# Cross-attention and feed-forward on one core: a new plan of the background work, products four tiles behind, a constant in the eviction of scores

## The chip, the cores and the metric

The kernel runs on one core of one Trainium2 chip. The metric is the device time of one execution in microseconds. Three runs of the kernel before took 1978.9, 1977.6 and 1969.8 us, median 1977.6. Engines are named as in the profile: PE is TensorE, PEld its weight loads, DVE VectorE, ACT ScalarE, POOL GpSimd, SP SyncE, which here only issues DMAs.

## The reference, cut to what matters

1600 query rows (16 x 100) attend to 5776 context rows (16 x 361) with 16 heads of 32. Queries and keys are quantised per row and head to 127 steps, values per column, and the softmax weights per row to 255 steps. A feed-forward part with 1408 hidden columns follows; the change does not touch it.

```python
def _fq_sym(x, axis):
    s = jnp.max(jnp.abs(x), axis=axis, keepdims=True) / 127.0
    s = jnp.maximum(s, 1e-08)
    return jnp.clip(jnp.round(x / s), -127.0, 127.0) * s      # value only
...
q, k, v = _fq_sym(q * scale, -1), _fq_sym(k, -1), _fq_sym(v, 2)  # v: over all keys
attn = softmax(einsum('bhqd,bhkd->bhqk', q, k))
attn = _fq_unsigned(attn, -1)                                  # 255 steps, s = max / 255
out = einsum('bhqk,bhkd->bhqd', attn, v)
...
x = x + xattn(layernorm(x), ctx) @ Wp + bp
x = x + ffn(x)
```

Because the largest weight of a row becomes 255, the weights in steps are exp(score - max + ln 255), rounded; the row's sum of the unrounded values is kept for the division at the end. So a row's maximum over all 5776 scores must be known before its first exponential.

## The kernel before, in words

**Stages.** A prologue (to 172.8 us) normalises and projects the queries, and projects, rounds and turns the keys and values of the first four heads. Then come 200 *tiles*, 172.8 to 1705.1 us, and then the feed-forward with the rest of the output projection, to 1972.7 us. A tile is 128 queries of one head against all keys: 12 tiles a head, and a thirteenth that holds the last 64 queries of two heads (25 tiles a pair of heads, 50 a *group* of four heads). The keys are padded to 5796 = 46 blocks (`NB`) of 126 (`KB`).

**A tile.** The loop at L1148 walks over the tiles. Each has five chunks of scores (`CHUNKS`, 1536, 1024, 1536, 1024, 656 columns in an even tile, the first four swapped in an odd one). For each chunk PE multiplies into one of two PSUM buffers `sl` (L1170), and DVE evicts it into one of two SBUF buffers `score` (L1186), multiplied by the row's negative scale `nqs`, which it reads through a pointer to a column of one element per partition, while it accumulates the minimum into `mx`. POOL makes of the five minima the bias `nb` (two instructions behind the fourth chunk, L1213 and L1214, and one behind the fifth, L1220). ACT takes the exponentials in two pieces (L1129): the first `NP` = 20 blocks go as bytes, those of two blocks packed in 16 bits, into `pairc`, at the end of the tile's own turn; the other 26 blocks as `codes` one tile later, at the place that `WINDOWS` calls "turn". SP issues the two DMA transposes (L1134 into `pk`, L1137 into `rT`) right behind each. POOL unpacks `pk` into `rU` (L1141) two tiles later. PE multiplies the transposed weights with the values (`av`, L1050, 46 blocks a tile) into `oacc`, `LAG` = 3 tiles behind; where in the tile how many blocks come stands in `WINDOWS`, whose entry per chunk is (turn, units of projection, blocks). `pk`, `rT` and `rU` have 2, 3 and 2 buffers.

**Background work.** While group g runs, the keys and values of group g+1 are made. `plan_pair` (L690) puts a pair of context blocks on tiles n and n+1: four projection matmuls a tile (`unit_pe`, L252, and L254 for the bias) into `pp`, one PSUM buffer; the loads of `cb` three blocks ahead (L217); the keys' maxima `pair_max` (L264, DVE) at the end of tile n+1; the copy of `pp` to SBUF, `pair_keep` (L275, ACT), ahead of the first exponential of tile n+1; then the scale (L281, POOL), its inverse (L287, DVE) and the rounding (L292, L298, POOL). 23 pairs take the 46 first tiles of a group. `plan_keys` puts the splitting of a head's keys into three bf16 parts (L360 to L366, POOL), their transposes (L373, PE) and the copy (L377, ACT) on the tiles that `PLAN["keys"]` lists. At the end of a group the values' maxima are taken over all keys (`values_max`, L305 and L309, DVE), turned and spread (L313 to L332), and the values divided (L337, POOL) and rounded (L340, ACT) on the tiles in `PLAN["divide"]`, some of them in the next group. `values_copy` (L392, POOL) makes a head's values f16. Finished heads are scaled into `og` (L1089) and stored (L1110, L1116). The last group has no next one to project: its tiles carry the output projection instead (`part_load` to `part_store`, L721 to L752, and the loads of the feed-forward's weights, L441).

**What sets the order.** Each engine executes in the order in which the program issues to it, and the order in the loop is written out by hand: per tile the lists "pool", "turn", "pe", "dve", "act0" and "act" hold what `put` placed there. "act0" runs ahead of the second exponential of the tile before, "act" ahead of the tile's own first exponential, "dve" behind the five evictions, "pool" ahead of everything that POOL does in the tile. The DMA queues in question are ACT's (loads of `cb`, weights, `qT`) and SP's (the transposes, `store`, the prologue's loads).

Of the kernel before, what the change touches and what calls it, by code (L numbers as in the profile page):

```python
# [22 lines left out]
P = 128  # L23
C = 512
H = 16
# [6 lines left out]
NP = 20  # L32
# [7 lines left out]
LAG = 3  # L40
# [9 lines left out]
    "keys": ((1, 3, 5, 7, 9, 11), (13, 15, 17, 19, 21, 23), (25, 27, 29, 31, 33, 35), (37, 39, 41, 43, 45, 48)),  # L50
    "query": ((0, 4, 5), (14, 14, 18), (25, 27, 29), (39, 41, 43)),
    "copy": ((4, 8), (18, 20), (29, 30), (50, 50)),
    "max": (30, 31, 33, 35, 37, 41, 40, 42, 45, 46),
    "finish": (47, 48, 49),
    "divide": (49, 52, 52, 52, 52, 52, 53, 53, 53, 54, 55, 56),
    "prefetch": (46, 47, 49, 49),
    "store": (3, 6, 9, 9),
# [4 lines left out]
    "keys": ((1, 3, 5, 7, 9, 11), (13, 15, 17, 19, 21, 23), (25, 27, 29, 31, 33, 35)),  # L62
    "query": ((0, 4, 5), (14, 14, 18), (25, 27, 29)),
    "copy": ((4, 8), (18, 20), (29, 30)),
# [17 lines left out]
    ((0, 0, 2), (1, 1, 8), (0, 1, 16), (0, 1, 8), (0, 1, 12)),  # L82
    ((0, 0, 0), (1, 0, 8), (0, 2, 8), (0, 1, 20), (0, 1, 10)),
# [4 lines left out]
    ("norm", 0), ("codes", 0), ("project", 1), ("keep", 0), ("norm", 1), ("values", 3), ("codes", 1),  # L88
# [24 lines left out]
def xattn_ffn(ctx: ExitStack, tc: tile.TileContext, xin, ctxt, wq, bq, wkv, bkv, wp, bp, w13, w2, nw, out):  # L113
# [100 lines left out]
    def load(g, t):  # L214
        if g < H // G and t < NB:
            cbs[g, t] = genp.tile([P, 4, P], F32, name=f"cb_{g}_{t}", tag="cb", bufs=3)
            nc.scalar.dma_start(cbs[g, t], ctxt[:, t])  # L217

    def prefetch(g, i):

        if i < 4:
            if i == 0:
                wts_g[g] = genp.tile([P, 4, 2 * P], F32, name=f"wkv_{g}", tag="wkv", bufs=1)
            nc.scalar.dma_start(wts_g[g][:, i, :], wkv[:, g, i, :])
        if i:
            load(g, i - 1)
# [62 lines left out]
    def keys_round(g, u):  # L289
# [8 lines left out]
        nc.gpsimd.tensor_scalar(kint[g][:, 2 * u : 2 * u + 2, :], vraw[:, k : k + 2, :], MAGIC, MAGIC, ALU.add, ALU.subtract)  # L298

    def values_max(g, t0, t1, c0=0, c1=P):  # L300

        if t0 == 0 and c0 == 0:
            fin["vm"] = genp.tile([P, P], F32, name=f"vm_{g}", tag="vm", bufs=1)
        vm = fin["vm"][:, c0:c1] if t0 == 0 else genp.tile([P, P], F32, name=f"vp_{g}_{t0}", tag="vp", bufs=1)
        nc.vector.tensor_reduce(  # L305
            vm, vraw[:, t0:t1, c0:c1].rearrange("p t c -> p c t"), AX.X, ALU.max, apply_absolute_value=True
        )
        if t0:
            nc.vector.tensor_tensor(fin["vm"], fin["vm"], vm, ALU.max)  # L309

    def values_turn(g, pool):
        fin["pt"] = pool.tile([P, P], F32, name=f"vmt_{g}", tag="tr")
        nc.tensor.transpose(fin["pt"], fin["vm"], ident_f)  # L313

    def values_scale(g):
        vmx = genp.tile([P, 1], F32, name=f"vmx_{g}", tag="vmx", bufs=1)
        nc.vector.reduce_max(vmx, fin["pt"], axis=AX.X)
# [4 lines left out]
    def values_diag(g):  # L322
        fin["diag"] = genp.tile([P, P], F32, name=f"diag_{g}", tag="vm", bufs=1)
        nc.gpsimd.tensor_scalar(fin["diag"], ident_f, fin["rsv"], None, ALU.mult)

    def values_spread(g, pool):
        fin["pb"] = pool.tile([P, P], F32, name=f"rsvb_{g}", tag="tr")
        nc.tensor.matmul(fin["pb"], ones_f, fin["diag"], start=True, stop=True)

    def values_keep(g):  # L330
        fin["rsvb"] = genp.tile([P, P], F32, name=f"rsvs_{g}", tag="vp", bufs=1)
# [49 lines left out]
    def query_load(h, c0=0, c1=NQ, copies=(0, 1, 2)):  # L381

        qT[h] = qTs[h % 2]
        for r in copies:
            nc.scalar.dma_start(qT[h][r * HD : (r + 1) * HD, c0:c1], q_dram[h * HD : (h + 1) * HD, c0:c1])
# [20 lines left out]
    def values_sum_keep(h):  # L406
# [5 lines left out]
        nc.scalar.dma_start(v16[h][0:1, NP:, :], exp_["row0", h])  # L412
# [5 lines left out]
    def values_rest_keep(h):  # L418
        nc.scalar.dma_start(v16[h][1:2, NP:, :], exp_.pop(("row1", h)))
# [40 lines left out]
    with (  # L460
# [135 lines left out]
        for t in range(NB):  # L596
# [11 lines left out]
            if t % 8 == 7 or t == NB - 1:  # L608
                c0 = t // 8 * 8
                at(t + WHEN["values"], values_max, 0, c0, t + 1)  # L610
# [24 lines left out]
        at(n, values_turn, 0, pps)  # L635
# [22 lines left out]
    for s in score:  # L658
        nc.gpsimd.memset(s[:, NK:], 1e30)
# [4 lines left out]
    with tc.manual_schedule():  # L664
# [25 lines left out]
        def plan_pair(g, u, n):  # L690
# [5 lines left out]
            put(n + 1, "act", pair_keep, g, u, first=True)  # L696
            put(n + 2, "pool", keys_scale, g, u)
            put(n + 2, "dve", keys_inverse, g, u)
            put(n + (4 if 12 < n % 50 < 35 else 3), "pool", keys_round, g, u)
# [249 lines left out]
        for g in range(H // G):  # L949
# [6 lines left out]
            if g == 0:  # L956
                put(2, "act", query_load, h, 8 * P, NQ)
                put(1, "turn", values_sum, h, psa)
                put(1, "act0", values_sum_keep, h)
                put(2, "pool", values_rest, h, first=True)  # L960
                put(2, "act0", values_rest_keep, h)
# [49 lines left out]
            for i in range(8):  # L1011
                put(base + PLAN["max"][i], "dve", values_max, g + 1, 0, 30, 16 * i, 16 * i + 16)
            put(base + PLAN["max"][8], "dve", values_max, g + 1, 30, 38)
            put(base + PLAN["max"][9], "dve", values_max, g + 1, 38, NB)
            n0, n1, n2 = (base + n for n in PLAN["finish"])
            put(n0, "turn", values_turn, g + 1, psa)
# [5 lines left out]
            put(n2, "pool", values_divide, g + 1, 0, NB, 0, HD)  # L1022
            put(n2, "act", values_round, g + 1, 0, NB, 0, HD)
            for i in range(12):
                n = base + PLAN["divide"][i]
                if i and g + 2 == H // G:
                    n = base + 51 + (i - 1) // 4
# [92 lines left out]
        def exponentials(which, i):  # L1120
            n, sc, nb = which
# [4 lines left out]
            else:  # L1126
# [3 lines left out]
                dst, src, AF.Exp, bias=nb, scale=-1.0, accum_out=usum[:, i, n % 50 : n % 50 + 1]  # L1130
            )
            if i == 0:
                pk = packed[n] = late.tile([P, NP // 2, P], U16, name=f"pk_{n}", tag="pk", bufs=2)
# [199 lines left out]
```

## Time and profile before

| what | before |
|---|---|
| three runs, median | 1977.6 us (1969.8 to 1978.9) |
| the profiled execution, its own time | 1974.55 us |
| its span | 1972.7 us |
| mean granted clock of TensorE | 0.956 |
| prologue | 0 to 172.8 us |
| groups one to four of 50 tiles | 378.6, 381.4, 383.1 and 389.2 us |
| feed-forward behind the tiles | 1705.1 to 1972.7 us |
| exponentials `codes`, mean | 3024 ns |
| exponentials `pairc`, mean | 2399 ns |
| unpacking `rU` (POOL), mean | 2318 ns |
| rounding of keys L298 (POOL), mean | 1100 ns |

The span runs from the first to the last instruction of the profiled execution. A row of the groups of instructions reads: line, engine, operation, output and input with their shapes, count, then busy time in us and the mean of one in ns, then the idle time of the engine just ahead of these instructions and what ended most of it. "(+2 forms)" says that the mean is over several shapes. A row of the timeline reads: start in us, duration, engine, line, operation, and in square brackets the wait and what ended it. A matmul pairs with its weight load, which has rows of its own under PEld.

### The profile page before, as it was taken

What the parts mean: (1) busy time and instruction counts of PE and PEld (TensorE: products, weight loads), DVE (VectorE), ACT (ScalarE), POOL (GpSimd) and SP (SyncE); (2) the same over time, 40 slices, a digit from 0 to 9 for tenths busy, and PEclk for the clock granted to TensorE, in tenths of its full rate; (3) what the DMA queues carried; (4) which work ended last, traced back from release to release, by engine and by line L of the source; (5) the groups of instructions that cost most, each with busy time, mean ns of one, the idle gap of its engine ahead of it and who ended that gap; (6) DMA issues with size and microseconds to landing.
All of it is one profiled execution on the core that took longest, in us unless ns stands there. A gap on an engine that the chain in (4) does not pass through costs nothing. (4 is left out here: it accounts for less than half of the span.)

```text
span 1972.7 us, 43743 instructions
## 1 busy us (share of the span) xinstructions
PE 1734.4 (88%) x16747; PEld 1151.0 (58%) x16747; DVE 1782.8 (90%) x2987; ACT 1448.3 (73%) x1492; POOL 1294.6 (66%) x1749
## 2 busy tenths in 40 slices
PE   7997899889788998897889988888888888789998
PEld 6884555555455555554555555544555555567785
DVE  7888999999999999999889999997899989788775
ACT  4445888888788888887888888877788878654443
POOL 5655777877688788776877787768666646352121
PEclk8998999999899999998999999988999889889999
DMA  4444999999899999998999999979999999830000
GB/s 150 137 134 81 198 209 201 199 197 200 160 188 194 209 205 203 205 194 153 189 195 205 201 207 204 187 137 170 194 199 194 188 205 207 188 108 27 27 30 19
DMA packets 1008089, 330.43 MB, mean 168 GB/s; under 512 B 965595, under 2 KB 971907, under 8 KB 1007878
## 3 DMA queue, kind: packets, MB, share of 16 engines
q1 hardware_dynamic: 972356, 266.24, 76.8%
q10 hardware_dynamic: 35522, 61.39, 11.7%
q8 instruction: 131, 2.15, 0.4%
q14 instruction: 80, 0.66, 0.1%
HBM read 79.15 MB, written 10.72 MB: 46 GB/s over the span
## 5 line engine op out<-in xcount | busy, mean ns | idle before, releaser
L1186 DVE TENSOR_SCALAR_CACHE_REDUCE score<-sl,nqs 128x1536 f32<-128x1536 f32 (+2 forms) x960 | 1309.9, 1417 | 88.8 <-PE sl L1170 69.5
L1170 PE MATMUL sl<-kT,qT 96*128 96x512 bf16 (+1 forms) x2304 | 643.0, 379 | 115.3 <-DVE score L1186 107.0
L1129 ACT ACTIVATE codes<-score,nb 128x3276 uint8<-128x3276 f32 x200 | 604.8, 3024 | 14.4 <-DVE score L1186 8.2
L1129 ACT ACTIVATE pairc<-score,nb 128x2520 uint8<-128x2520 f32 x200 | 479.8, 2399 | 176.1 <-POOL nb L1220 146.4
L1141 POOL CAST rU<-pk 128x2560 f16<-128x2560 uint8 x200 | 463.5, 2318 | 39.9 <-DMA pk<-pairc 28.3
L252 PE MATMUL pp<-wkv,cb 128*128 128x256 f32 x1104 | 335.9, 396 | 1.2 <-ACT vraw L275 1.1
L1170 PEld LDWEIGHTS <-qT 96*128 96x128 bf16 x2304 | 186.9, 97 | 229.3 <-issue 167.4
L1050 PEld LDWEIGHTS <-rT 128*128 128x128 f16 x4992 | 204.9, 97 | 194.4 <-DMA rT<-codes 95.0
L1050 PE MATMUL oacc<-v,rT 128*128 128x32 f16 x4992 | 216.5, 178 | 67.8 <-DMA rT<-codes 62.9
L252 PEld LDWEIGHTS pp<-wkv,cb 128*128 128x128 f32 x1104 | 195.5, 193 | 71.0 <-issue 8.9
L1050 PEld LDWEIGHTS <-rU 128*128 128x128 f16 x3840 | 132.1, 96 | 48.9 <-issue 12.1
L890 POOL TENSOR_TENSOR rw<-rl,nw_b 128x480 f32<-128x480 f32 (+3 forms) x39 | 49.5, 1270 | 164.4 <-ACT rl L889 81.1
L1050 PE MATMUL oacc<-v,rU 128*128 128x32 f16 x3840 | 156.7, 177 | 0.0
L1213 POOL TENSOR_SCALAR m<-mx 128x1 f32<-128x1 f32 x200 | 73.6, 368 | 114.2 <-DVE score L1186 113.4
L1214 POOL TENSOR_SCALAR m<-m,mx 128x1 f32<-128x1 f32 x200 | 57.0, 285 | 121.6 <-DVE score L1186 113.7
L872 PE MATMUL p<-w13h,hT 128*128 128x480 f32 (+3 forms) x312 | 123.3, 395 | 4.6 <-ACT hT L857 4.0
L872 PE MATMUL p<-w13l,hT 128*128 128x480 f32 (+3 forms) x312 | 121.2, 389 | 3.2 <-POOL w13l L454 2.8
L1220 POOL TENSOR_SCALAR nb<-mx,m 128x1 f32<-128x1 f32 x200 | 58.6, 293 | 83.3 <-DVE score L1186 46.0
L298 POOL TENSOR_SCALAR kb<-vraw 128x256 bf16<-128x256 f32 x92 | 101.2, 1100 | 8.4
L377 ACT COPY kT<-kt 96x1008 bf16<-96x1008 bf16 x96 | 90.6, 943 | 10.7 <-PE kt L373 10.7
L275 ACT COPY vraw<-pp 128x512 f32<-128x512 f32 x69 | 40.3, 584 | 74.8 <-DVE am L264 74.8
L292 POOL TENSOR_TENSOR vraw<-vraw,rs 128x256 f32<-128x256 f32 x92 | 59.2, 644 | 44.6 <-DVE rs L287 32.7
(219 smaller groups left out, 2676.7 us busy)
## 6 DMA issues: line engine op xcount, KB each, us to landing
cb<-in ACTq DMA_DIRECT2D x138, 256.0 KB
cr<-in SPq DMA_DIRECT2D x46, 256.0 KB
qT<-q_dram ACTq DMA_DIRECT2D x45, 100.0 KB
pk<-pairc SPq DMA_TRANSPOSE x200
rT<-codes SPq DMA_TRANSPOSE x200
xn<-in ACTq DMA_DIRECT2D x12, 256.0 KB
x_s<-in ACTq DMA_DIRECT2D x12, 256.0 KB
x_dram<-x_s ACTq DMA_DIRECT2D x12, 256.0 KB
```

The source lines that it names most:

```text
L252: nc.tensor.matmul(pp, cbs[g, t][:, kb, :], wts_g[g][:, kb, :], start=(kb == 0), stop=False)
L292: nc.gpsimd.tensor_tensor(kv, kv, batch.pop(("rs", g, u)).rearrange("p t h -> p (t h)").unsqueeze(2).broadcast_to([P, 2 * G, HD]), ALU.mult,)
L298: nc.gpsimd.tensor_scalar(kint[g][:, 2 * u : 2 * u + 2, :], vraw[:, k : k + 2, :], MAGIC, MAGIC, ALU.add, ALU.subtract)
L377: nc.scalar.copy(kT[h][:, c0 * KB : (c0 + n) * KB].rearrange("p (b k) -> p b k", k=KB), exp_.pop(("pt", h, c0))[:, :n, 2:])
L872: nc.tensor.matmul(pt[:r, :w], T["h", t][:, kb, :r], last_w[c][p][:, i * 4 + kb, :], start=(kb == 0 and p == 0), stop=(kb == 3 and p == 1),)
L1050: nc.tensor.matmul(oacc[h][:, t, :], turned(n, bl), v16[h][:, bl, :], start=(bl == turns[0]), stop=(bl == turns[-1]),)
L1129: nc.scalar.activation(dst, src, AF.Exp, bias=nb, scale=-1.0, accum_out=usum[:, i, n % 50 : n % 50 + 1])
L1141: nc.gpsimd.tensor_copy(r.rearrange("p (b two) q -> p b two q", two=2), packed.pop(n).bitcast(U8).rearrange("p b (q two) -> p b two q", tw ...
L1170: nc.tensor.matmul(sl[:, x0:x1], qT[h][:, t * P : (t + 1) * P], kT[h][:, col + x0 : col + x1], start=True, stop=True,)
L1186: nc.vector.tensor_scalar(sc[:, col : col + w], sl[:, :w], s2, None, ALU.mult, ALU.min, accum_out=mx[:, c : c + 1])
L1213: nc.gpsimd.tensor_scalar(m1, mx[:, 0:1], mx[:, 1:2], mx[:, 2:3], ALU.min, ALU.min)
L1220: nc.gpsimd.tensor_scalar(nb, mx[:, 4:5], m1, LN255, ALU.min, ALU.add)
```

## The change

It does the following:

- **Eviction.** The multiplication by `nqs` in the eviction becomes one by the constant 1.0 and the accumulation a maximum; the padding of `score` becomes -1e30. The factor moves to the exponentials, where `scale` is now a pointer to `qs` instead of the constant -1, and to `nb`, which is now the maximum times `nqs` plus ln 255. On POOL one instruction for the first three maxima stands behind the fourth chunk, and two behind the fifth.
- **Lag.** `LAG` goes from 3 to 4, the unpacking from two to three tiles behind, `pk` gets a third and `rT` a fourth buffer. Behind the tiles, one more tile of products and one more unpacking remain.
- **Split of blocks.** `NP` goes from 20 to 22: `pairc` has 22 blocks, `codes` 24.
- **Keys.** `pair_keep` moves from the end of tile n+1 to "act0" of tile n+2: it stands behind the first exponential of tile n+1 and ahead of the second. The rounding with `MAGIC` is two POOL instructions that add, where it was one that adds and subtracts, and it always stands in tile n+3.
- **Maxima of the values.** They go into four rows of `tops`, which are turned one by one and reduced together; L309 falls away.
- **Plan.** Splits of keys start on even tiles, copies of values, maxima, divisions and stores on other tiles; the divisions reach to tile 60 (that is 10 of the next group), with a list of their own ahead of the last group. `WINDOWS` for the first three groups moves the projection's units and the blocks of products; `LAST["windows"]` stays.
- **Loads.** Within the tiles `cb`, the projection's weights, `qT` and the two rows of v16 are issued by SP instead of ACT. The last group's own loads stay on ACT.

```diff
-NP = 20
+NP = 22
-LAG = 3
+LAG = 4
...
-    "keys": ((1, 3, 5, 7, 9, 11), (13, 15, 17, 19, 21, 23), (25, 27, 29, 31, 33, 35), (37, 39, 41, 43, 45, 48)),
+    "keys": ((0, 2, 4, 6, 8, 10), (12, 14, 16, 18, 20, 22), (24, 26, 28, 30, 32, 34), (38, 40, 42, 44, 46, 48)),
-    "copy": ((4, 8), (18, 20), (29, 30), (50, 50)),
-    "max": (30, 31, 33, 35, 37, 41, 40, 42, 45, 46),
-    "finish": (47, 48, 49),
-    "divide": (49, 52, 52, 52, 52, 52, 53, 53, 53, 54, 55, 56),
+    "copy": ((9, 11), (19, 21), (31, 33), (50, 50)),
+    "max": (
+        *((31 + i, 0, 0, 30, 16 * i, 16 * i + 16) for i in range(8)),
+        (39, 1, 30, 38, 0, 64), (40, 1, 30, 38, 64, P), (44, 2, 38, 44, 0, 64), (45, 2, 38, 44, 64, P), (46, 3, 44, NB),
+    ),
+    "finish": (47, 48, 49, 49),
+    "divide": (51, 51, 51, 51, 53, 53, 55, 55, 57, 57, 59, 60),
+    "end": (50, 51, 51, 51, 51, 51, 52, 52, 53, 53, 53, 53),
-    "store": (3, 6, 9, 9),
+    "store": (2, 5, 8, 8),
...
 WINDOWS = (
-    ((0, 0, 2), (1, 1, 8), (0, 1, 16), (0, 1, 8), (0, 1, 12)),
-    ((0, 0, 0), (1, 0, 8), (0, 2, 8), (0, 1, 20), (0, 1, 10)),
+    ((0, 0, 4), (1, 0, 8), (0, 2, 10), (0, 1, 12), (0, 1, 12)),
+    ((0, 1, 8), (1, 1, 4), (0, 1, 10), (0, 1, 12), (0, 0, 12)),
 )
...
-            nc.scalar.dma_start(cbs[g, t], ctxt[:, t])
+            (nc.sync if live else nc.scalar).dma_start(cbs[g, t], ctxt[:, t])
...
-        nc.gpsimd.tensor_scalar(kint[g][:, 2 * u : 2 * u + 2, :], vraw[:, k : k + 2, :], MAGIC, MAGIC, ALU.add, ALU.subtract)
+        raw = vraw[:, k : k + 2, :]
+        nc.gpsimd.tensor_scalar(raw, raw, MAGIC, 1.0, ALU.add, ALU.mult)
+        nc.gpsimd.tensor_scalar(kint[g][:, 2 * u : 2 * u + 2, :], raw, -MAGIC, 1.0, ALU.add, ALU.mult)
+    tops = genp.tile([P, 4, P], F32, name="tops")
+    def values_max(g, i, t0, t1, c0=0, c1=P):
         nc.vector.tensor_reduce(
-            vm, vraw[:, t0:t1, c0:c1].rearrange("p t c -> p c t"), AX.X, ALU.max, apply_absolute_value=True
+            tops[:, i, c0:c1], vraw[:, t0:t1, c0:c1].rearrange("p t c -> p c t"), AX.X, ALU.max, apply_absolute_value=True
         )
-        if t0:
-            nc.vector.tensor_tensor(fin["vm"], fin["vm"], vm, ALU.max)
...
             put(n + 1, "dve", pair_max, g, u)
-            put(n + 1, "act", pair_keep, g, u, first=True)
+            put(n + 2, "act0", pair_keep, g, u)
             put(n + 2, "pool", keys_scale, g, u)
             put(n + 2, "dve", keys_inverse, g, u)
-            put(n + (4 if 12 < n % 50 < 35 else 3), "pool", keys_round, g, u)
+            put(n + 3, "pool", keys_round, g, u)
...
-            put(n2, "pool", values_divide, g + 1, 0, NB, 0, HD)
-            put(n2, "act", values_round, g + 1, 0, NB, 0, HD)
+            for n, t0, t1 in ((n2, 0, NB // 2), (n3, NB // 2, NB)):
+                put(n, "pool", values_divide, g + 1, t0, t1, 0, HD)
+                put(n, "act", values_round, g + 1, t0, t1, 0, HD)
             for i in range(12):
-                n = base + PLAN["divide"][i]
-                if i and g + 2 == H // G:
-                    n = base + 51 + (i - 1) // 4
+                n = base + PLAN["end" if g + 2 == H // G else "divide"][i]
...
-                dst, src, AF.Exp, bias=nb, scale=-1.0, accum_out=usum[:, i, n % 50 : n % 50 + 1]
+                dst, src, AF.Exp, bias=nb, scale=s1, accum_out=usum[:, i, n % 50 : n % 50 + 1]
...
-                pk = packed[n] = late.tile([P, NP // 2, P], U16, name=f"pk_{n}", tag="pk", bufs=2)
+                pk = packed[n] = late.tile([P, NP // 2, P], U16, name=f"pk_{n}", tag="pk", bufs=3)
-            r = rTs[n, 1] = late.tile([P, NB - NP, P], F16, name=f"rT_{n}", tag="rT", bufs=3)
+            r = rTs[n, 1] = late.tile([P, NB - NP, P], F16, name=f"rT_{n}", tag="rT", bufs=4)
...
-            if n > 1:
-                unpack(n - 2)
+            if n > 2:
+                unpack(n - 3)
...
                 nc.vector.tensor_scalar(
-                    sc[:, col : col + w], sl[:, :w], s2, None, ALU.mult, ALU.min, accum_out=mx[:, c : c + 1]
+                    sc[:, col : col + w], sl[:, :w], 1.0, None, ALU.mult, ALU.max, accum_out=mx[:, c : c + 1]
                 )
...
-                    nc.gpsimd.tensor_scalar(m1, mx[:, 0:1], mx[:, 1:2], mx[:, 2:3], ALU.min, ALU.min)
-                    nc.gpsimd.tensor_scalar(m1, m1, mx[:, 3:4], None, ALU.min)
+                    nc.gpsimd.tensor_scalar(m1, mx[:, 0:1], mx[:, 1:2], mx[:, 2:3], ALU.max, ALU.max)
...
-            nc.gpsimd.tensor_scalar(nb, mx[:, 4:5], m1, LN255, ALU.min, ALU.add)
+            nc.gpsimd.tensor_scalar(m2, mx[:, 3:4], mx[:, 4:5], m1, ALU.max, ALU.max)
+            nc.gpsimd.tensor_scalar(nb, m2, s2, LN255, ALU.mult, ALU.add)
...
-        unpack(NTI - 2)
-        unpack(NTI - 1)
+        for i in (3, 2, 1):
+            unpack(NTI - i)
```

## The prediction

> **What bounds the kernel now.** First the page: no engine is idle enough to be ignored, and VectorE (DVE) leads.
>
> ```profile
> PE 1734.4 (88%) x16747; PEld 1151.0 (58%) x16747; DVE 1782.8 (90%) x2987; ACT 1448.3 (73%) x1492; POOL 1294.6 (66%) x1749
> L1186 DVE TENSOR_SCALAR_CACHE_REDUCE score<-sl,nqs 128x1536 f32<-128x1536 f32 (+2 forms) x960 | 1309.9, 1417 | 88.8 <-PE sl L1170 69.5
> ```
>
> The eviction of scores, five per tile and 1000 in all, takes two thirds of the span, and stood idle only 88.8 us. Next the view by stretches. The 200 tiles run from 172.8 to 1705.1 us; these are the second group of 50 tiles, which also projects the next heads, and the last, which does not:
>
> ```profile
> 551.40:932.80 381.40, 334.41 (x3698) 212.05 (x3698) 364.91 (x565) 317.00 (x274) 297.36 (x425) 0.97 1.08 195
> 1315.90:1705.10 389.20, 333.62 (x3600) 202.99 (x3599) 350.66 (x524) 308.04 (x265) 246.57 (x334) 0.92 1.06 196
> ```
>
> After the length come busy PE, PEld, DVE, ACT, POOL, granted clock, DMA share, GB/s. DVE is busy 96% of the second group: there it is the bound. The timeline of one regular even tile shows how near the others stand:
>
> ```profile
> 305.95 0.42 DVE L264 TENSOR_REDUCE am<-pp 128x8 f32<-128x256 f32 x1
> ...
> 306.29 1.81 DVE L1186 TENSOR_SCALAR_CACHE_REDUCE score<-sl,nqs 128x1536 f32<-128x1536 f32 x1
> ...
> 306.41 0.59 ACT L275 COPY vraw<-pp 128x512 f32<-128x512 f32 x1 [1.38 <-DVE am L264]
> ...
> 306.56 0.29 POOL L1220 TENSOR_SCALAR nb<-mx,m 128x1 f32<-128x1 f32 x1
> 306.89 2.40 ACT L1129 ACTIVATE pairc<-score,nb 128x2520 uint8<-128x2520 f32 x1
> ...
> 307.05 0.70 PE L252 MATMUL pp<-wkv,cb 128*128 128x256 f32 x2
> ...
> 308.16 0.81 PE L1170 MATMUL sl<-kT,qT 96*128 96x512 bf16 x3 [0.22 <-DVE score L1186]
> ...
> 309.64 0.59 PE L1170 MATMUL sl<-kT,qT 96*128 96x512 bf16 x2
> ...
> 310.97 1.28 DVE L1186 TENSOR_SCALAR_CACHE_REDUCE score<-sl,nqs 128x1024 f32<-128x1024 f32 x1
> ```
>
> The tile's evictions start at 306.29, 308.02, 309.23, 310.97 and 312.17, and the next tile's at 313.29: 7.00 us; that odd tile takes 7.05 (to 320.34), a pair 14.05. The copy that frees `pp` ends at 307.00, and the matmul into the next `pp` starts 0.05 later. The scores for the fourth eviction are complete at 310.23, only 0.74 before they are taken.
>
> What is above 7.03 us a tile is extra DVE work and waits:
>
> ```profile
> PEld L1050 <- DMA rT<-codes: 95.0, 73, 4.7
> DVE score L1186 <- PE sl L1170: 69.5, 103, 3.5
> ```
>
> Asked tile by tile, DVE's idle time in those tiles where PE waited over 0.8 us for rT adds up to 44 us: 22 in the first three groups, 22 in the last.
>
> **The change part by part.**
>
> *Constant in the eviction.* What a scalar read through a pointer costs on DVE, from rows one with and one without it:
>
> ```profile
> L919 DVE TENSOR_SCALAR kb<-kb,tiny 128x640 f32<-128x640 f32 x12 | 7.6, 630 | 0.0
> L920 DVE TENSOR_SCALAR gq<-kb 128x640 bf16<-128x640 f32 x12 | 6.8, 564 | 0.6
> L847 DVE TENSOR_SCALAR inv<-tiny 128x1 f32<-128x1 f32 x12 | 2.6, 214 | 0.4
> L848 DVE TENSOR_SCALAR inv<-inv 128x1 f32<-128x1 f32 x12 | 1.8, 154 | 0.4
> ```
>
> 630-564=66, 214-154=60. The eviction of 1536 takes 1813 ns by form, 1600 at an element per 1/0.96 ns and 213 beside, as the single element with a pointer. I take 60 ns off each start-to-start distance: 0.30 us a tile, a pair 13.45. Bounds 0 (the pointer is fetched under the previous eviction) and 66. [...]
>
> *The factor moves to the exponentials* (L1129). ACT's rows give 299 ns beside the elements with one pointer (2399 for 2520 at 0.827 ns, the slope to 3024 for 3276), and 200 for the square L901 without (600 for 480). A second pointer is put at 95 ns, twice a tile; NP=22 moves 252 elements from one to the other and adds nothing. ACT has 65 us idle in the second group against 50 x 0.19 = 9.5: hidden. The first exponential, with its 252 elements, lasts 2.40+0.21+0.09=2.70.
>
> *Maxima on POOL.* Before, one operation followed the last eviction; now two (m2, 0.37 as L1213; nb, 0.29). From the accumulator's end (306.04): 0.17 to start, 0.37, 0.09, 0.29, 0.04: the exponential starts 0.96 later, that is 0.71 after the next tile's first eviction.
>
> *The copy of projected keys and values moves behind that exponential*, one tile later. It then starts 0.71+2.69 after the even tile's first eviction, ends at 3.99, and PE's first projection matmul, now behind the third scores in program order, waits from about 2.6 to 4.04. Queued behind it on PE: the second matmul, ten blocks of products, the fourth scores: 0.53+0.25+0.59, so these are there at 5.41, DVE starts at 5.5 instead of 4.50. The new wait costs **1.0 us a pair**: 14.45 against 14.05. Bounds: 0, if the matmul waits for nothing, and 1.4, PE's whole wait. With 23 pairs in three groups: 69 x 0.40 = **+27.6**.
>
> *Maxima in rows.* Per group before: 8 x 0.96 + 2 x 1.915 + 2 x 0.85 = 13.2 us (L305, L309). After: the same eight, 2 x 1.0 and 2 x 0.8 by 2 ns an element, 0.55: 11.8. Six stand at the end of odd tiles (5.6 us) and postpone the first eviction but not the exponential, so they fill the new wait: 6.2 count. 3 x -7.0 = **-21**.
>
> *Tiles without projections*, 4 in each of three groups and 50: 62 x -0.30 = **-18.6**.
>
> *LAG 4, unpack three behind, a buffer more.* rT has one tile more, about 7 us, and the longest wait was 4.7: **-44**; bounds 0 and -69.5.
>
> *POOL.* Unpacking 2816 instead of 2560: 0.23 us a tile; m2's second pointer 0.08; the rounding (L298, 1100 ns) becomes two operations, each between 405 (the cast of 256, L361) and 1260 (twice the 128 of L324, 631): 0.9, the middle of rows that are alike in engine and shape, +0.7 a pair. A pair's POOL time goes from 11.4 (the split L360 to L366 2.8; the scale L281 0.28; L292 and L298 together 1.74; twice the unpacking 2.32; twice the maxima 0.95) to 12.7, with 17 hand-overs of 0.07 about 13.9: under 14.45. Where copies or divisions of values come on top it is late; the divisions are spread to tile 60, which relieves the transitions, where DVE sat idle some 5 us a group: both together **-2**, bounds -10 and +25.
>
> *Loads by SP.* SP issues per tile rT (3.88) and pk (1.5), with a load (0.33) 5.7 of 7 us. A load waits for matmuls of its own tile, which end before the exponential that pk, next behind it, waits for: nothing, at most 0.5 a tile if that cover goes, and with LAG 4 nothing waits for it. ACT's issues ran under its exponentials: no gain.
>
> *Ends.* A fourth tile of products (46 x 0.025) and a third unpacking in the tail, one rounding more ahead: **+3**.
>
> The profiled execution took 1974.55 (span 1972.7 and 1.85 around it), 3 under the median of three runs. 1974.6+27.6-21-18.6-44-2+3 = **1919.6**, predicted as 1920.
>
> **The rivals.**
>
> *The copy holds nobody up.* Then pairs gain 0.60 each and the maxima 1.4 a group: 1974.6-41.4-4-18.6-44-2+3 = **1868**. For it: before, the matmul waited 1.2 us in all for copies; against it: the order on ACT and 0.74 us of slack.
>
> *POOL becomes the bound*: rounding at 1260 twice makes a pair's POOL time 14.6, so that every copy, division and correction of the group (some 9 us beyond what its slack takes) comes on top: 1920+3 x 9 = **1947**. Against it: DVE waits in that pair anyway.
>
> *The pointer cost nothing*: pairs 14.05+0.82 (the third eviction ends 0.18 later), 69 x 0.82=56.6, no 18.6: 1974.6+56.6-21-44-2+3 = **1967**.
>
> *Slower: the new wait drops PE's clock.* A row of the last group:
>
> ```profile
> 1488.40:1491.80 3.40, 2.63 (x41) 1.97 (x40) 3.40 (x6) 3.40 (x5) 2.57 (x3) 1.00 0.73 45
> 1491.80:1494.10 2.30, 1.23 (x24) 0.83 (x23) 2.30 (x3) 2.30 (x3) 0.36 (x1) 1.00 1.18 315
> 1494.10:1501.00 6.90, 6.40 (x30) 3.18 (x30) 5.42 (x10) 6.39 (x5) 5.50 (x9) 0.51 1.19 249
> ```
>
> PE idle 0.77 and 1.07 us in two short stretches, and the clock stands at 0.51 for 6.9 us, in which DVE is idle 1.5. A hole of 1.4 us in every pair could do that each time: 69 x 1.3 more, about **2010**. It decides from three pairs in four on: 52 x 1.3 = 67 puts 1920 at 1987, half a per cent over the median; 34 x 1.3 = 44 still gives 1964. Against it: at 409.6 to 416.6 PE was idle 1.33 us at clock 1.00. [...]
>
> *The change hides nothing*: waits for rT only move, 1920+44 = **1964**.
>
> **How the numbers follow.** The forecast 0.38 (own range 1895 to 1945); copy harmless 0.19; POOL 0.10; pointer free or waits only moved 0.10, of which half falls within 0.5% of 1977.6, the other half below; slower clock, or a POOL so late that it costs as much, 0.17; a sum of small losses that ends within 0.5% 0.06. Under 1858 I leave 0.08 (the first rival with the better bounds of POOL and transitions); over 2000, 10 short of the slower rival's own figure, 0.12: range 1858 to 2000. A measurement of this kernel can tell 0.5%, 10 us: faster 0.38+0.19+0.10+0.05 = 0.72, same 0.05+0.06 = 0.11, slower 0.17.
>
> **What would show it.** Eviction of 1536 at 1.75 us instead of 1.81; in an even tile the projection's first matmul with idle time ended by ACT vraw, and the fourth eviction idle about 1 us ended by PE; waits for rT near nothing; the two rounding rows near 0.9; the clock over 0.95 in the first three groups. If regular pairs take 13.5 the first rival holds; if over 15 at a lower clock, the slower one. Wrong altogether if pk or rT, now queued with loads on SP, land later than their tile of slack.

## The result, and the profile after

The changed kernel takes 2127.1 us (median of four runs, one of them disturbed and left out of the ratio), the kernel before 1978.3 us: 1.074 of its time, 95% interval 1.0675 to 1.0805. Its profiled execution took 2124.8 us, with a span of 2123.0. The prediction said 1920, with 2000 as the upper end of its range. The kernel became slower by 149 us where the prediction had it faster by 58.

The page of the profile after, its lines on busy time, the granted clock and three groups of instructions:

```profile
PE 1825.4 (86%) x16734; PEld 1198.6 (56%) x16734; DVE 1730.4 (82%) x2982; ACT 1482.4 (70%) x1495; POOL 1318.0 (62%) x1844
...
PEclk9997888898888988888779899888899999989999
...
L1185 DVE TENSOR_SCALAR_CACHE_REDUCE score<-sl 128x1536 f32<-128x1536 f32 (+1 forms) x1000 | 1316.5, 1357 | 293.1 <-PE sl L1169 257.7
...
L1130 ACT ACTIVATE pairc<-score,nb,qs 128x2772 uint8<-128x2772 f32 x192 | 518.6, 2701 | 334.1 <-POOL nb L1222 327.7
...
L257 PE MATMUL pp<-wkv,cb 128*128 128x256 f32 x1104 | 412.9, 474 | 77.4 <-ACT vraw L280 73.2
```

DVE is no longer the bound: it stands idle 293 us ahead of the evictions, where it was 89, and in 258 of them waits for PE. The last row shows two things at once; in the page before it read:

```profile
L252 PE MATMUL pp<-wkv,cb 128*128 128x256 f32 x1104 | 335.9, 396 | 1.2 <-ACT vraw L275 1.1
```

The projection's matmul now waits 73 us for the copy `vraw` (L280, `pair_keep`), where it waited 1.1, and its mean went from 396 to 474 ns though it is the same matmul. The work is the same, so the clock is the suspect; the rows below show it.

By stretches (length, busy PE, PEld, DVE, ACT, POOL, granted clock, DMA share, GB/s): the second group of tiles, the last group, and the feed-forward.

```profile
608.20:1046.50 438.30, 370.23 (x3698) 230.10 (x3696) 351.37 (x567) 324.18 (x274) 302.62 (x447) 0.86 0.86 166
1488.60:1855.70 367.10, 321.33 (x3623) 199.07 (x3622) 335.81 (x524) 313.60 (x264) 258.90 (x333) 0.94 1.10 200
1855.70:2123.00 267.30, 243.66 (x1339) 190.58 (x1335) 206.59 (x450) 127.67 (x277) 76.60 (x58) 0.97 0.19 52
```

The second group takes 438.3 instead of 381.4 us at a clock of 0.86 instead of 0.97. The last group, which projects nothing, gains: 367.1 instead of 389.2. The feed-forward stays (267.3, before 267.6), the prologue is 2.3 longer. So the three groups that project lost 170.4 us (1313.5 instead of 1143.1), and all else won 20.

One even tile of the first group, in time order (start, duration, engine, line, idle time and what ended it):

```profile
258.36 1.75 DVE L1185 TENSOR_SCALAR_CACHE_REDUCE score<-sl 128x1536 f32<-128x1536 f32 x1
...
259.04 2.70 ACT L1130 ACTIVATE pairc<-score,nb,qs 128x2772 uint8<-128x2772 f32 x1 [0.84 <-POOL nb L1222]
...
260.17 0.81 PE L1169 MATMUL sl<-kT,qT 96*128 96x512 bf16 x3 [1.22 <-DVE score L1185]
...
261.74 0.56 ACT L280 COPY vraw<-pp 128x512 f32<-128x512 f32 x1
...
262.35 1.27 PE L257 MATMUL pp<-wkv,cb 128*128 128x256 f32 x4 [1.37 <-ACT vraw L280]
...
263.73 1.01 PE L1169 MATMUL sl<-kT,qT 96*128 96x512 bf16 x2
264.54 1.06 PE L257 MATMUL pp<-wkv,cb 128*128 128x256 f32 x2
264.78 1.23 DVE L1185 TENSOR_SCALAR_CACHE_REDUCE score<-sl 128x1024 f32<-128x1024 f32 x1 [1.84 <-PE sl L1169]
```

This is the wait that the prediction described, nearly to the digit: the copy behind the first exponential ends at 262.30, 3.94 after the tile's first eviction (3.99 was forecast). But it does not stand alone. PE has just waited 1.22 us for the first eviction, then 1.37 for the copy, and in the 3.41 us from 258.94 to 262.35 it worked 0.81. What comes then runs slowly: two score matmuls take 1.01 where in other tiles they take 0.59, two projection matmuls 1.06 instead of 0.60. The tile lasts 10.00 us, the odd one behind it 6.80. An idle stretch of PE is called a hole below, and a stretch at half clock (granted 0.50, as from 263.21 to 266.62 us here) a drop.

### The profile page after: what moved, and what is told of

It is laid out like the page before. It is cut to its first block, busy times and chain, and to the rows that moved or that the text cites. A ratio compares the mean times of both kernels' runs of the same rounds, so it can differ in the third digit from the quotient of the medians.

```text
span 2123.0 us, 43762 instructions
## 1 busy us (share of the span) xinstructions
PE 1825.4 (86%) x16734; PEld 1198.6 (56%) x16734; DVE 1730.4 (82%) x2982; ACT 1482.4 (70%) x1495; POOL 1318.0 (62%) x1844
## 5 line engine op out<-in xcount | busy, mean ns | idle before, releaser
L1185 DVE TENSOR_SCALAR_CACHE_REDUCE score<-sl 128x1536 f32<-128x1536 f32 (+1 forms) x1000 | 1316.5, 1357 | 293.1 <-PE sl L1169 257.7
L1130 ACT ACTIVATE pairc<-score,nb,qs 128x2772 uint8<-128x2772 f32 x192 | 518.6, 2701 | 334.1 <-POOL nb L1222 327.7
L1130 ACT ACTIVATE codes<-score,nb,qs 128x3024 uint8<-128x3024 f32 x192 | 558.7, 2910 | 8.5 <-DMA rT<-codes 8.4
L1142 POOL CAST rU<-pk 128x2816 f16<-128x2816 uint8 x200 | 505.9, 2529 | 7.6 <-DMA pk<-pairc 3.5
L257 PE MATMUL pp<-wkv,cb 128*128 128x256 f32 x1104 | 412.9, 474 | 77.4 <-ACT vraw L280 73.2
L257 PEld LDWEIGHTS pp<-wkv,cb 128*128 128x128 f32 x1104 | 236.6, 232 | 199.5 <-ACT vraw L280 110.5
L1221 POOL TENSOR_SCALAR m<-mx,m 128x1 f32<-128x1 f32 x200 | 71.9, 360 | 388.7 <-DVE score L1185 196.3
L1185 DVE DVE_READ_ACCUMULATOR score<-sl 128x1 f32 x1000 | 82.6, 83 | 0.0
L377 PEld LDWEIGHTS <-stack 128*96 128x96 bf16 x736 | 55.2, 126 | 34.0 <-POOL stack L370 8.1
L377 PE MATMUL kt<-ident_b,stack 128*96 128x128 bf16 x736 | 58.8, 223 | 14.3 <-POOL stack L370 7.9
```

What stands on the lines that cost most here:

```text
L257: nc.tensor.matmul(pp, cbs[g, t][:, kb, :], wts_g[g][:, kb, :], start=(kb == 0), stop=False)
L377: nc.tensor.transpose(pt[:, b, :], st[:, b, :], ident_b)
L1130: nc.scalar.activation(dst, src, AF.Exp, bias=nb, scale=s1, accum_out=usum[:, i, n % 50 : n % 50 + 1])
L1142: nc.gpsimd.tensor_copy(r.rearrange("p (b two) q -> p b two q", two=2), packed.pop(n).bitcast(U8).rearrange("p b (q two) -> p b two q", tw ...
L1185: nc.vector.tensor_scalar(sc[:, col : col + w], sl[:, :w], 1.0, None, ALU.mult, ALU.max, accum_out=mx[:, c : c + 1])
L1221: nc.gpsimd.tensor_scalar(m2, mx[:, 3:4], mx[:, 4:5], m1, ALU.max, ALU.max)
```

## The experiments

All are compared with the kernel before, run beside them; "e1" and so on name them further on. Times are medians.

**e1: the copy back at its old place, all else as changed.**

```diff
-            put(n + 2, "act0", pair_keep, g, u)
+            put(n + 1, "act", pair_keep, g, u, first=True)
```

> The changed kernel with the copy of projected keys and values (pair_keep) back at its old place, ahead of the first exponential of tile n+1; all else as changed. Theory (the copy's new place makes a hole on PE in every even tile, and the hole halves PE's clock): even tiles fall from 10.19 us on average to about 6.85, 69 x 3.3 = 230 us less: about 1897, between 1885 and 1925, clock over 0.95 in the first three groups. Rival (the hole only shows what the new plan, the loads on SP or POOL's longer chain cause): over 2050, with even tiles still far longer than odd ones.

Measured: 1946.1 us, 0.983 of the time before (0.978 to 0.987). The move of this one copy costs 181 us; the rest of the change, taken together, gains 34. But it is 49 us more than the theory had. Even tiles fall from 10.19 to 7.77 us on average, not 6.85. A regular even tile of e1 has no wait for the copy any more:

```profile
705.04 1.75 DVE L1185 TENSOR_SCALAR_CACHE_REDUCE score<-sl 128x1536 f32<-128x1536 f32 x1
...
706.85 0.81 PE L1169 MATMUL sl<-kT,qT 96*128 96x512 bf16 x3 [1.22 <-DVE score L1185]
707.50 1.03 PE L257 MATMUL pp<-wkv,cb 128*128 128x256 f32 x4
...
711.96 1.22 DVE L1185 TENSOR_SCALAR_CACHE_REDUCE score<-sl 128x1024 f32<-128x1024 f32 x1 [0.32 <-issue]
```

The projection starts right behind the scores, but the 1.22 us ahead of them stay. They come from the new windows, which give PE 12 blocks of products and no projection ahead of the third scores, where the old ones gave it 10 blocks and a unit of projection. By stretches of 3.4 us in e1, first one regular tile, then a tile behind a maximum of values (two neighbouring stretches):

```profile
705.04:708.45 3.41, 2.19 (x21) 1.50 (x20) 3.41 (x6) 3.41 (x4) 2.83 (x8) 1.00 0.96 211
```

```profile
788.43:791.84 3.41, 1.57 (x4) 0.93 (x4) 2.93 (x6) 3.41 (x4) 2.95 (x7) 0.72 0.97 219
791.84:795.29 3.45, 3.45 (x34) 2.40 (x32) 2.92 (x5) 3.19 (x4) 2.96 (x3) 0.79 1.24 235
```

In the regular tile PE is busy 2.19 of 3.41 us and the clock is full. A maximum on DVE (0.98 us) lengthens the hole to 2.13 us, the clock falls, and the tile takes 8.54 us instead of 6.92.

**e2: the copy at its new place, the projection moved behind it.**

```diff
-    ((0, 0, 4), (1, 0, 8), (0, 2, 10), (0, 1, 12), (0, 1, 12)),
+    ((0, 0, 4), (1, 0, 8), (0, 0, 20), (0, 2, 8), (0, 2, 6)),
```

> The changed kernel, copy at its new place; in even tiles the third window holds 20 blocks of products and no projection, the four units stand in the fourth and fifth windows (2 with 8 blocks, 2 with 6). Theory (the wait for the copy holds up what PE has behind it): PE comes to the first unit at about 4.0 us after the tile's first eviction, the copy ends at 3.7, so nothing waits: 1890 to 1935. If the place on ACT alone costs (copy behind one exponential, next exponential behind the copy) and not PE's wait: over 2050.

Measured: 1997.5 us (1.009, 1.006 to 1.013): 130 us better than the change, 60 us short of the theory. PE still waits for the copy 52 times, and a regular even tile that keeps the full clock takes 7.64 us, since now four units of projection crowd behind the fourth scores. Most of the harm goes when nothing that waits for the copy stands ahead of the fourth scores. But the edit also puts more products into the hole, and 30 of 60 even tiles keep the clock, so it does not tell the wait's price from the clock's.

**e3: the hole filled.**

```diff
+                if n < NTI - 50 and n % 2 == 0 and c in (1, 2) and quarters:
+                    fill = psa.tile([P, C], F32, name=f"fill_{n}_{c}", tag="tr")
+                    for _ in range(3 if c == 1 else 5):
+                        nc.tensor.matmul(fill, ident_b[0 : 3 * HD, :], kT[h][:, 0:C], start=True, stop=True)
                 for _ in range(units):
```

> The changed kernel with eight matmuls more in every even tile that projects (3 ahead of the products in the second window, 5 ahead of the units in the third), into a PSUM buffer that nothing reads: the wait for the copy stays, the hole is filled. It separates the wait from the clock. Theory (wait about 1.0 us a pair, the rest is the halved clock): clock over 0.95, even tiles 7.8 to 8.3, 69 x 2.1 = 145 less: about 1980, between 1950 and 2010. If the clock was no part of it: 2120 or more. If the wait costs nothing once the clock holds: 1900 to 1930.

Measured: 2068.3 us (1.045, 1.042 to 1.049). The clock came back (mean 0.950), and a regular even tile takes 8.57 us at full clock, somewhat above the theory's 7.8 to 8.3; and the total is 58 us above the theory's range: seventeen tiles of the three groups take 11.5 to 15.4 us. The buffer of the added matmuls is also that of the transposes and the values' sums, which may be why; no run shows it.

**e4 and e5: the kernel before with the new windows, with and without the copy's new place.**

```diff
 WINDOWS = (
-    ((0, 0, 2), (1, 1, 8), (0, 1, 16), (0, 1, 8), (0, 1, 12)),
-    ((0, 0, 0), (1, 0, 8), (0, 2, 8), (0, 1, 20), (0, 1, 10)),
+    ((0, 0, 4), (1, 0, 8), (0, 2, 10), (0, 1, 12), (0, 1, 12)),
+    ((0, 1, 8), (1, 1, 4), (0, 1, 10), (0, 1, 12), (0, 0, 12)),
 )
...
-            put(n + 1, "act", pair_keep, g, u, first=True)
+            put(n + 2, "act0", pair_keep, g, u)
```

Both have the windows; the last two lines are e4's alone.

> The kernel before with only the copy at its new place and the new windows for the first three groups. Theory: 69 pairs get about 3 us longer, 1978 + 200 = 2180, between 2120 and 2220, clock under 0.9 in the first three groups. Rival (the copy does no harm without the rest of the change): 1960 to 2000.

> The kernel before with only the new windows for the first three groups, the control for e4_before_copy_moved. Theory (the copy's place is what cost 200 us there): 1960 to 2010; the new windows leave PE idle 1.2 us in the first part of every even tile, so a few more drops of the clock, some 15 us more than before. Rival (the windows themselves cost what e4 showed): over 2100.

Measured: e4 2182.7 us (1.104, 1.099 to 1.109), e5 2012.2 us (1.016, 1.012 to 1.020). The copy's place costs 170 us in the kernel before as well, so it needs no part of the change but the windows for that. No run has the copy at its new place with the old windows, so what the place alone costs is not shown. The windows alone cost 30, twice what was expected.

**e6, e7, e8: e1 with loads issued by ACT, with the windows of before, with both.**

```diff
-            (nc.sync if live else nc.scalar).dma_start(cbs[g, t], ctxt[:, t])
+            nc.scalar.dma_start(cbs[g, t], ctxt[:, t])
...
 WINDOWS = (
-    ((0, 0, 4), (1, 0, 8), (0, 2, 10), (0, 1, 12), (0, 1, 12)),
-    ((0, 1, 8), (1, 1, 4), (0, 1, 10), (0, 1, 12), (0, 0, 12)),
+    ((0, 0, 2), (1, 1, 8), (0, 1, 16), (0, 1, 8), (0, 1, 12)),
+    ((0, 0, 0), (1, 0, 8), (0, 2, 8), (0, 1, 20), (0, 1, 10)),
 )
```

The first edit, with the same for wkv, qT and the rows of v16, is e6's and e8's, the second e7's and e8's.

> The version e1_copy_back with the loads of the tiles issued by ACT again. In e1, PE waits 1.75 us for wkv in the first tile of a group and that tile and the next take 11.6 and 10.8 us where the kernel before takes 7.0 and 8.2, and in tile 4 PE waits 4.0 us for a row of v16. Theory (SP issues its loads late, behind its transposes): 8 us less at each of two starts of groups and 4 in the first group, 1946 - 20 = 1926 (1915 to 1935). Rival (the loads are late for another reason, or ACT loses as much): 1940 to 1955.

> The version e1_copy_back with the windows of the kernel before in the first three groups. Theory (the new windows leave a hole of 1.2 us in every even tile; where a maximum of values makes it 2.1 us, the clock halves, 1.7 us each in some 6 tiles of a group; and a unit behind the fifth scores makes the next tile's first scores 0.3 us late): 18 x 1.7 + 69 x 0.3 = 51 less, about 1895 (1880 to 1915). Rival (the drops come from the maxima and stay whatever the windows): 1935 to 1950.

> The version e1_copy_back with both: the loads issued by ACT and the windows of the kernel before. Theory: the two gains add, 1946 - 51 - 20 = 1875 (1860 to 1900), under the kernel before by 4 to 6%.

Measured: e6 1944.4 (0.983, 0.978 to 0.988), e7 1925.8 (0.974, 0.970 to 0.978), e8 1928.1 (0.974, 0.971 to 0.977). The windows gave 20 us, not 51: the drops of the clock behind the maxima are all but gone (in tiles 32 to 40 of a group 1 of 15 even tiles has one, in e1 12), but a pair of regular tiles still takes 13.74 us (e1 13.73). The issuer of the loads makes no difference in the total: e6's first tile of a group takes 6.95 us instead of 11.6, but the next keeps 10.7, and in e8 PE's wait in the first tiles has only moved by one tile, to where POOL makes four divisions in a row. The prediction's "no gain" for the loads stood, though not for its reason.

**e9, e10, e11: one part of e7 undone.**

```diff
-LAG = 4
+LAG = 3
...
-                    sc[:, col : col + w], sl[:, :w], 1.0, None, ALU.mult, ALU.max, accum_out=mx[:, c : c + 1]
+                    sc[:, col : col + w], sl[:, :w], ones_f[:, 0:1], None, ALU.mult, ALU.max, accum_out=mx[:, c : c + 1]
...
-        nc.gpsimd.tensor_scalar(raw, raw, MAGIC, 1.0, ALU.add, ALU.mult)
-        nc.gpsimd.tensor_scalar(kint[g][:, 2 * u : 2 * u + 2, :], raw, -MAGIC, 1.0, ALU.add, ALU.mult)
+        nc.gpsimd.tensor_scalar(kint[g][:, 2 * u : 2 * u + 2, :], raw, MAGIC, MAGIC, ALU.add, ALU.subtract)
```

The three edits are those of e9 (there with the unpacking and the buffers of pk and rT as before), e10 and e11.

> The version e7_old_windows (copy and windows as before, 1926) with the products three tiles behind and the unpacking two, pk and rT with 2 and 3 buffers as before. Theory (the fourth tile of lag took away the waits for rT): waits for rT return and cost 44 us as the prediction had it: 1970 (1950 to 1985). Rival (the waits only moved elsewhere): 1918 to 1936.

> The version e7_old_windows with the eviction's constant 1.0 read through a pointer to a column of ones; the result is the same. Theory (60 ns for each of 1000 evictions, where DVE is the bound): the eviction of 1536 at 1813 ns instead of 1753, and 35 to 60 us more: 1961 to 1986. Rival (DVE's waits take most of it up): under 1950.

> The version e7_old_windows with the rounding of keys as one POOL instruction that adds and subtracts. In the changed kernel the two instructions take 408 and 413 ns, together less than the one's 1100. Theory (POOL is not the bound): 1926 within 8 us, L298's row back at 1100 ns. Rival (POOL's 0.28 us a pair matter where it runs late): 1935 to 1950.

Measured: e9 1981.9 us (1.000, 0.998 to 1.002), e10 1965.5 (0.991, 0.988 to 0.995), e11 1931.4 (0.974, 0.969 to 0.979). The lag is worth some 55 us, the constant some 39, the rounding nothing that can be told. Undoing the lag brought PE's waits for rT back: 49.4 us ahead of its weight loads against 6.1 in e7. The eviction of 1024 elements takes 1280 ns with the pointer (1221 without), as in the kernel before.

**e12: e8 with the divisions spread out.**

```diff
-    "divide": (51, 51, 51, 51, 53, 53, 55, 55, 57, 57, 59, 60),
+    "divide": (52, 53, 53, 54, 54, 55, 55, 56, 56, 57, 57, 58),
```

> The version e8_both (copy, windows and issuer of loads as before, 1928) with the divisions of values spread over tiles 52 to 58 instead of four in tile 51: there tile 101 took 15.3 us, POOL busy with four divisions and ACT with four roundings ahead of the copy that PE's transposes wait for. Theory: 8 us less at each of two starts of groups: about 1912 (1900 to 1920). Rival (the work only moves to the next tiles): 1923 to 1933.

Measured: 1932.0 us (0.975, 0.970 to 0.980), no gain over e8: the work only moved. In this plan the next group's first copies overwrite some blocks of values ahead of their division, so part of its values aren't the reference's; it is read for its time alone.

**e13: the changed kernel, the first hole filled and the second left.**

```diff
+                if n < NTI - 50 and n % 2 == 0 and c == 1 and quarters and not todo["turn"]:
+                    fill = psa.tile([P, C], F32, name=f"fill_{n}_{c}", tag="tr")
+                    for _ in range(4):
+                        nc.tensor.matmul(fill, ident_b[0 : 3 * HD, :], kT[h][:, 0:C], start=True, stop=True)
                 for _ in range(units):
```

> The changed kernel with four matmuls more in an even tile that projects, into a buffer that nothing reads, in the second window alone: there PE waits 1.2 us for the first eviction anyway, so they delay nothing, and the wait for the copy behind them stays whole. It tells the price of the wait from that of the clock without the delays that the five matmuls of e3_filled brought. Theory (a stretch of 3.4 us in which PE is busy under half halves the clock of the next): PE busy about 0.65 in that stretch, clock 1.00 in nearly all even tiles, these at 8.3 to 8.6 us, and 2030 to 2070. Rival (the clock falls whatever is filled in, by the wait itself): over 2100, even tiles at 10.

Measured: 2084.1 us (1.055, 1.051 to 1.060), above the range of the theory and below the rival's: it caught the clock in a third of the tiles only. So one run now holds even tiles of both kinds, with the same instructions. Two of them, first by stretches (the clock stands behind the busy times), then the first projection matmul and DVE's fourth eviction of each:

```profile
801.10:811.10 10.00, 8.27 (x68) 5.00 (x67) 6.77 (x13) 6.42 (x6) 7.19 (x13) 0.83 0.94 178
817.89:826.47 8.58, 6.84 (x68) 4.28 (x67) 6.69 (x13) 6.17 (x5) 6.91 (x12) 1.00 0.98 187
```

```profile
805.02 1.17 PE L257 MATMUL pp<-wkv,cb 128*128 128x256 f32 x4 [1.37 <-ACT vraw L280]
...
807.35 1.22 DVE L1185 TENSOR_SCALAR_CACHE_REDUCE score<-sl 128x1024 f32<-128x1024 f32 x1 [1.74 <-PE sl L1169]
...
821.82 1.13 PE L257 MATMUL pp<-wkv,cb 128*128 128x256 f32 x4 [1.38 <-ACT vraw L280]
...
823.67 1.22 DVE L1185 TENSOR_SCALAR_CACHE_REDUCE score<-sl 128x1024 f32<-128x1024 f32 x1 [1.27 <-PE sl L1169]
826.40 1.22 DVE L1185 TENSOR_SCALAR_CACHE_REDUCE score<-sl 128x1024 f32<-128x1024 f32 x1 [0.62 <-PE sl L1169]
```

Both wait some 1.37 us for the copy; the second keeps the clock and takes 8.58 us, the first loses it and takes 10.00. Sorted by the trace's clock, with the tiles 12 and 14 of each group and the first of a group left out, 20 even tiles without a drop have a mean of 8.51 us and 40 with one 10.10 (e3, with eight matmuls more instead of four: 49 without, 8.60). In the changed kernel 58 of 60 have a drop (mean 10.23), in e1 19 of 60 (8.86), the other 41 take 7.08.

**e16: the kernel before with the constant alone.**

```diff
-                    sc[:, col : col + w], sl[:, :w], s2, None, ALU.mult, ALU.min, accum_out=mx[:, c : c + 1]
+                    sc[:, col : col + w], sl[:, :w], 1.0, None, ALU.mult, ALU.max, accum_out=mx[:, c : c + 1]
```

The factor in the exponentials, `nb`, `m1`, `m2` and the padding follow the change.

> The kernel before with the constant in the eviction alone (with what it needs: maxima instead of minima, the factor in the exponentials, two POOL instructions behind the fifth chunk). Theory (60 ns an eviction where DVE is the bound; e10 showed 39 us): 1978 - 39 = 1939 (1925 to 1955). Rival (with the waits for rT of the kernel before in place, the gain goes into these): 1960 to 1980.

Measured: 1969.3 us, 0.997 of the time before (0.993 to 1.000): by the ratio 7 us less, by its interval between 14 us less and no gain at all, so the rival was right. The waits in its trace, next to the 95.0 us of the kernel before:

```profile
PEld L1050 <- DMA rT<-codes: 139.4, 104, 5.3
```

With faster evictions PE waits for rT 104 times instead of 73. The author's reading is that three tiles are shorter and the transposes come no sooner; how long the transposes took here was not shown. Beside the longer lag the constant is worth 39 us (e10); with the shorter one hardly a gain can be told from noise.

## Why the prediction was wrong, point by point

**The step that failed: the price of the new wait, and that the clock was left to a rival.** The prediction named the move of the copy, its order on ACT, what queues behind the matmul on PE, and its size: "the new wait costs 1.0 us a pair". By itself the wait costs 8.51 - 7.08 = 1.4 us, the upper bound of the prediction; between the regular tiles shown it is 8.58 - 6.92 = 1.7. Both compare e13 with e1, whose even tiles lack the four added matmuls. The missing part is in the last rows of e13 above: DVE waits not only 1.27 us at the fourth eviction but 0.62 at the next tile's first, because the units of projection behind the held matmul come late as well. In e1, without the wait for the copy, it waits 0.32 there, so 0.3 are new. The prediction stopped at the fourth scores. The larger error was the clock. "Slower: the new wait drops PE's clock" was a rival at 0.17, at 1.3 us a pair, a figure for which the prediction gives no working. It came true in 58 of 60 tiles, at 10.10 - 8.51 = 1.6 us each (1.4 between the two tiles shown), where the sum had nothing. The two account for what the copy costs: e1 itself has the drop in 19 of 60 tiles, so 1.4 + 1.6 x (58 - 19) / 60 = 2.4 us an even tile, and 10.19 - 7.77 = 2.42 was measured; times 69 is 167 of the 181 us between e1 and the change.

**Why the clock was misjudged.** The evidence against that rival was one stretch with 1.33 us of idle PE at full clock, the evidence for it one row at half clock. Cut into steps of 3.41 us from one change of the granted clock to the next (the last section tells why), the two are alike: PE is busy 2.33 us from 408.66 to 412.07, where the clock stays, and 2.34 from 1490.69 to 1494.10, where it falls behind. So neither could tell what a larger hole does: in the tile of the change shown above PE is busy 1.67 us of such a step, from 259.80 to 263.21. For the wait comes on top of a hole that the new windows make just ahead: PE waits 1.22 us for the first eviction, works 0.81, then waits 1.37 (the rows shown). These two idle pieces, 2.6 us together and neither over 1.37, were followed by a step at 0.50. The prediction priced what the wait delays, and did not add up PE's idle time in the three microseconds around it. From the windows of the diff this could be had: no projection and 12 blocks ahead of the third scores.

**The copy harmless (the first rival, 1868).** It is e1 with 1946.1, or e7 with 1925.8 where the new windows are taken out too: 58 us short. Of this, 20 us are in regular pairs: 13.74 us instead of 13.45, 69 x 0.29. The rest is spread over the starts of groups (in e7 four of the five tiles 47 to 51, around the first change of groups, take 8.9 to 13.4 us, before none over 8.3), over the last group, which in e7 gained 25 us where 37 were counted, and the prologue; these were not told apart.

**The constant.** Its size was right: the eviction of 1536 takes 1752 ns (forecast 1.75 us, before 1813), and odd tiles went from 7.05 to 6.79. The rows of before give (1813 - 1280) / 512 = 1.04 ns an element between the evictions of 1024 and 1536, and those after the same, (1752 - 1221) / 512, so the 59 to 61 ns saved do not grow with the elements. That the pointer cost nothing was the rival at 1967; e10 decides against it: with the pointer the eviction of 1536 takes 1812 ns again. What it is worth depends on the lag: 39 us with the longer one, 7 without, between none and 14 (e16).

**The lag.** Forecast 44 us with bounds 0 and 69.5, measured 55. In the changed kernel the waits for rT ahead of PE's weight loads are gone (95.0 before, 1.0 after).

**The rounding.** Forecast 0.9 us for each of the two instructions, 0.7 more a pair on POOL; measured, they took 408 and 413 ns, at the lower bound of the prediction (405) and together less than the one with its 1100. The sign was wrong, and nothing hung on it (e11).

**Maxima in rows.** A pair of the old reductions (2 x 1.9) and of `tensor_tensor` (2 x 0.85) left, as counted. That the maxima "fill the new wait" came true in the changed kernel. In its even tiles 32 to 40 of a group, where the tile ahead ends with a maximum, DVE waits 1.26 us for the fourth scores on average, in the even tiles 16 to 30 without maxima 2.40, and the odd tile ahead and the even one together take 17.11 us instead of 17.45. Without the wait, in e1, the same maxima lengthen PE's hole and cost clock: 16.05 instead of 14.01, with a drop in 12 of 15 even tiles instead of 1 of 24. The rest of the plan shows no gain: e9, which has all of the change but the lag, the copy and the windows, takes 1.000 of the time before (0.998 to 1.002), the constant alone 0.997 (0.993 to 1.000).

## What to carry to other kernels

Before an instruction is moved behind a long one on its engine, add up the idle time that PE will have in the three or four microseconds around the new wait, holes that were there already included, and not only the wait; where PE works less than half of that time, count the halved clock as the forecast and not as a rival (here it followed in 54 of 54 such steps of the changed kernel and in 7 of 8 of the kernel before). Follow the late engine's queue past the next tile's first instruction: here 0.3 us of the wait's price stood there. And price two gains together when one shortens a period and the other gives a transfer more time (rT, whose issues before took 4.32 us in the median): here they were worth 39 and 55 us beside each other, and the first 7 alone, not clear of noise.

## What the runs showed of the hardware

The granted clock of TensorE changed in these traces on a grid of 3.413 us: all stretches at half clock (0.50) in the records are one, two or more of these long, but for the last of each, which the end cuts. With the traces cut along that grid, between the third tile and the end of the third group, stretches at full clock in which PE was busy less than half were followed by a half-clock one in 7 of 8 cases in the kernel before, in 54 of 54 in the changed one, 22 of 22 in e1 and 8 of 8 in e7. Busy 50 to 65%, it went either way (19 of 24 in the changed kernel, 9 of 45 in e1); above 70% it never happened in these four, and 4 times in 4015 stretches in all sixteen traces. So in these traces a hole cost or did not by where it fell on the grid. The two tiles of e13 above agree with it: PE is busy 1.77 us (52%) in the step from 802.56 to 805.98, behind which the clock halves, and 2.03 us (60%) in the step from 819.63 to 823.04, behind which it stays. A row of holes kept in step with the grid: in the changed kernel the clock is 0.50 for 3.41 us from 263.21, 280.28 and 297.34 us, five steps apart, while a pair of tiles takes 16.8.

A POOL instruction of 128 x 256 that adds and subtracts took 1092 ns (e11; 1100 before), one that adds and multiplies 408, or 413 where it writes bf16 as the first does (the change).
